# Two attention layers with a routed feed-forward: constants ahead of the statistics, the second late job's rows among the first one's gates, routing scatters one by one in two groups of four

## Chip, cores and metric

The kernel runs on one core of a Trainium2 chip. The metric is the device time of one execution in microseconds (us); lower is better. The core has a tensor engine (TensorE, PE in the profile; its weight loads are PEld), a vector engine (VectorE, DVE), a scalar engine (ScalarE, ACT), GpSimd (POOL) and a sync engine (SyncE, SP) that mostly issues DMAs. Each engine works through its own instruction list in order and waits on semaphores for the others. ScalarE, SP and GpSimd can issue DMAs; indirect ones, which take row numbers from a tile, are issued by GpSimd alone.

## What is computed

The reference, cut to what matters. `x` is (8, 512, 256) in float32, the context (8, 64, 256); there are 16 heads of 16, 8 experts with 1024 inner units and two experts for each token.

```python
x = x + L0_xattn(layernorm(x), ctx, ctx)       # 16 heads, softmax over 64 keys
x = x + L0_ffn(layernorm(x))                   # per batch, the 384 tokens with the highest
                                               # score get gelu(x @ w_block), the others pass
x = x + L1_xattn(layernorm(x), ctx, ctx, mask)
x = x + L1_ffn(layernorm(x))

def L1_ffn(hidden):                            # routed experts
    probs = softmax(x @ gate_w.T)
    w, idx = top_k(probs, 2); w = w / sum(w)
    for e in range(8):
        g, u = split(x @ gate_up[e].T)
        acc += combine[:, e] * ((silu(g) * u) @ down[e].T)
```

## The kernel before

The work has two halves. In the **front half** eight batches of 512 tokens go through a chain of steps each: attention 0, the token-choice layer, attention 2, and routing. A step is a Python closure that issues a few instructions on several engines, and a long string, `ORDER`, written out by hand, says which chain issues its next step: a digit 0 to 7 is the next step of that batch, a letter A to H the ranks of a batch, `s` the next setup step (constants, sorted by a number), `k` and `v` keys and values, `l` the job lists, `j` early expert jobs. `in_order` (L1215) ties every instruction behind the one before it on the same engine, so each engine's list follows `ORDER`. Only TensorE, VectorE, ScalarE and GpSimd are tied so; SP takes its DMAs in the order in which they are traced.

A normalisation (`norm_steps`, L375) has four steps. `stats` runs the statistics of four 128-token tiles on VectorE (L384, L385), adds eps (L387) and lets GpSimd raise to the power -0.5 (L389, `rstd`, with the constant `mhalf`). `scaled` makes `shift` on VectorE (L395) and four ScalarE activations (L398). Two `turned` steps transpose on TensorE (L413) against the constant `ident` and copy on ScalarE. Batch 0's chain needs these first; `keys` (L323, L331) needs the constant `headm`, which VectorE sums from `ownh` (L244). `mhalf`, `ownh`, `ident` and `minus` are made by GpSimd from nothing but fills and index patterns. GpSimd also issues the two loads of `bv`, the value biases, at the start of its list (L149), and adds the output bias `bo` to x (L435).

An attention's score part has a single PSUM buffer `ps_s`: `by_keys` fills `st` (L498, L506), two ScalarE exponentials `ex` (L515) empty it, and the next `st` can only then be filled. `by_tokens` uses the same buffer for `sc` (L466, L475), which VectorE's maximum (L482) empties.

Routing (`route_steps`, L698) ends in `placed`, which works out two slots for each token, and in four steps `sent_off(t)`, each with two indirect DMAs (L816, the "scatters"): 128 rows of 260 floats, from `xr` to the list `xs` in DRAM, for each token tile and each of the two choices. So a batch has eight. The last of a batch is made to wait until the other seven have landed and then stands for all, except in the last batch, whose eight are all waited for. Where `ORDER` has them, a batch's four steps stand next to each other or a few steps apart. Behind the scatters on GpSimd's list stand the next `rstd`s and `bo` additions.

Some experts' jobs run early (`early_steps`, L1069), woven into the last batches: rows and weights are loaded on SP, `gate_up` (L1138) and `down` (L1165) run on TensorE, and the rows are added to the output by indirect DMAs (`add_rows`, L106). Their first row load waits for the last scatter of batch 3.

In the **second half** 35 jobs follow (and a 36th if the counts need it), of three kinds: full (256 rows), one (128 rows), pair (two units of 64). For each the rows `xg` come by DMA (L1278), `enter` transposes them (L1318), copies `xjT` on ScalarE (L1320) and prepares tokens and weights on VectorE (L1324 to L1338); `gate_up_full` runs eight blocks of eight products each (L1349) with ScalarE's silu (L1357) and VectorE's product (L1358); `down` runs the second matrix (L1406) and adds the rows. For job i of the list, the gates come first, then `enter` of job i+1, then `down` of job i-1. At i = 0 there is no job before, so the transposes of job 1 stand directly ahead of job 1's gates. The steps of the first three jobs are tied by `in_order` too (`placed`, L1445). Job 0's rows are loaded behind its gate weights on SP and wait for all eight scatters of batch 7.

Of the kernel before, what the change touches and what calls it, by code (L numbers as in the profile page):

```python
# [47 lines left out]
NQ = P // QR  # L48

ORDER = """  # L50
sssss0sss0ksk0s1020001s0k110s1vs0s031010s7s2s40v320v2410030v20120ss01040502A010A30A0As10
1013010343201130005s12010sk0112151761Bs2B1BB112120241201v102s2050223s022302412C22123C2C0
21C02131012110323150030sv02411033123104102523105200004331323426D14D34Ds14D2341v233613421
63233344212345412615434311432513431414312E25124E544E452356E54722434237252346535264345645
256352452F362F2325F63F464556355473355463574536743566474353567335566346v37l64763G464jj77j
5jGj666j5j7jj47Gjjj765j7457j4G5j64654j7j6556747j5j76446444j4746sH6jj56j557j76j7j57jj7Hsj
76jjjjHH7565j65jj676jj7jj6j57j5j6j75557j555jj57j6j667j7jjjs67j66j76j7676j66j76s667j676jj
jj7jjj77j7j7jjjjj77jjs7j7j7j7j7j77jj7jjjljj7jj7jj
"""


# [1 line left out]
def xattn_ffn_kernel(ctx: ExitStack, tc: tile.TileContext, a: dict, out: bass.AP):  # L63
# [28 lines left out]
    def after(i, others):  # L92
        for other in others:
            tc.add_manual_dep(
                i, other.name,
                mybir.DependencyInfo(mybir.DependencyClass.Sync, mybir.DependencyReason.DATA),
                reason="rows that it needs",
            )

    def apart(i, others, reason):  # L100
        for other in others:
            tc.declare_no_dep(i, other, reason=reason)
# [14 lines left out]
    with ExitStack() as front:  # L117
# [36 lines left out]
        def load_layer(l, names, q):  # L154
            for n in names:
                how = load_mat if n[0] == "w" else load_col if n in ("bk", "bq") else load_row
                layers[l][n] = how(q, f"{n}{l}")
# [10 lines left out]
            q.dma_start(x_sb[:, t, :], x_t[0][:, t, :])  # L168
        load_layer(0, ("bk", "wv", "bq"), nc.scalar)
        load_layer(1, ("wv",), nc.sync)  # L170
        load_layer(0, ("bv",), nc.gpsimd)
        load_layer(1, ("bv",), nc.gpsimd)
        load_layer(0, ("wq", "bo", "wo"), nc.sync)
        nc.sync.dma_start(x_sb[:, TB : 2 * TB, :], x_t[1])
        load_layer(1, ("wk", "bk"), nc.sync)
# [42 lines left out]
        def within(at, name, shape, bounds, lasts=False):  # L218
# [12 lines left out]
            return v  # L231

        every = slice(0, P)
        mhalf = within(-0.9, "mhalf", [TB], [])
        setups.append((-0.89, lambda: nc.gpsimd.tensor_scalar_mul(mhalf, mhalf, -0.5)))

        ownh = within(
            -0.85, "ownh", [HC],
            [(ALU.is_ge, 0, [[-DK, HC]], 1), (ALU.is_ge, DK - 1, [[DK, HC]], -1)],
        )  # L240
        headm = const.tile([P, 2], F32, name="headm")
        setups.append((
            -0.84,
            lambda: nc.vector.tensor_reduce(  # L244
                headm, ownh.rearrange("p (r i) -> p i r", i=2), AX.X, ALU.add
            ),
        ))
        setups.append((-0.8, lambda: make_identity(nc, ident)))
        warm = const.tile([P, TB], F32, name="warm")
        setups.append((-0.895, lambda: nc.scalar.activation(warm, mhalf, AF.Exp)))  # L250

# [446 lines left out]
        def route_steps(b):  # L698
# [107 lines left out]
                    nc.vector.tensor_reduce(xr[:, :, D + col], part, AX.X, ALU.add)  # L806
                got["slots"] = slots

            def sent_off(t):
                slots, xr = got["slots"], got["xn"]  # L810

                sent = scattered.setdefault(b, [])
                for k in range(TOPK):
                    i = nc.gpsimd.indirect_dma_start(  # L816
                        out=xs,
                        out_offset=bass.IndirectOffsetOnAxis(ap=slots[:, t, k : k + 1], axis=0),
                        in_=xr[:, t, :],
                        in_offset=None,  # L820
                    ).ins
                    final = len(sent) == TB * TOPK - 1 and b < B - 1
                    if b >= B // 2:
                        apart(i, early_loads, "rows of other batches")
                    for other_i in sent:
                        if final:
                            tc.add_manual_dep(
                                i, other_i.name,
                                mybir.DependencyInfo(
                                    mybir.DependencyClass.Sync, mybir.DependencyReason.DATA  # L830
                                ),
                                reason="the last scatter stands for all",
                            )
                        else:
                            tc.declare_no_dep(i, other_i, reason="rows of their own")
                    sent.append(i)
                routed[:] = sent[-1:] if b < B - 1 else sent

            steps += [gates, logits, chosen, counted, weighed, placed]
            return steps + [lambda t=t: sent_off(t) for t in range(TB)]  # L840

# [225 lines left out]
        def early_steps(j):  # L1069
            got = {}  # L1070

            def load():
                if not e_w:
                    e_w["gu"] = wpool[0].tile([P, NC, 2 * FF], F32, tag="wgu", name="e_wgu")
                    e_w["dn"] = wpool[0].tile([P, NF, D], F32, tag="wdn", name="e_wdn")
                with tc.issue_after(last.pop().ins) if last else nullcontext():
                    row = nc.sync.value_load(
                        jobs_early[0:1, 0, j : j + 1], min_val=0, max_val=E * QROWS - P
                    )
                    e = nc.sync.value_load(jobs_early[0:1, 1, j : j + 1], min_val=0, max_val=E - 1)  # L1080
                i = nc.sync.dma_start(
                    e_xg, xs[bass.ds(row, 2 * P), :].rearrange("(s p) w -> p s w", p=P)
                ).ins
                early_loads.append(i)

                for b in scattered:
                    if b >= B // 2:
                        apart(i, scattered[b], "rows of other batches")
                after(i, scattered[B // 2 - 1][-1:])
                got["e"] = e  # L1090

            def load_piece(n):
# [117 lines left out]
            mybir.EngineType.PE, mybir.EngineType.DVE, mybir.EngineType.Activation,  # L1210
            mybir.EngineType.Pool,
        )
        behind = {}

        def in_order(step):  # L1215
            traced = nc.cur_bb.bb.instructions
            last = traced[-1].name
            step()
            made = []
            for i in reversed(nc.cur_bb.bb.instructions):  # L1220
                if i.name == last:
                    break
                made.append(i)
            for i in reversed(made):
                if i.engine not in engines:
                    continue
                ahead = behind.setdefault(i.engine, [])
                for other in ahead:
                    tc.add_manual_dep(
                        i, other,  # L1230
                        mybir.DependencyInfo(
                            mybir.DependencyClass.NoSync, mybir.DependencyReason.DATA
                        ),
                        reason="the order of the steps",
                    )

                if "DMA" not in type(i).__name__:
                    ahead.clear()
                ahead.append(i.name)
# [98 lines left out]
        nc.vector.tensor_tensor(wt[:, 0:subs], wt[:, 0:subs], wt2[:, 0:subs], ALU.add)  # L1338
        return xT, tok, wt

    def gate_up_full(j, xT, w):
        wgu = w[0][0]
        hT = moe.tile([P, NF, 2 * P], F32, tag="hT", name=f"hT_{j}")
        for f in range(NF):
            ps = ps_gu.tile([P, 2, 2 * P], F32, tag="gu", name=f"gu_{j}_{f}")
            for half in range(2):
                o = half * FF + f * P
                for c in range(NC):
                    nc.tensor.matmul(  # L1349
                        ps[:, half, :],  # L1350
                        lhsT=wgu[:, c, o : o + P],
                        rhs=xT[:, c].rearrange("p s q -> p (s q)"),
                        start=(c == 0),
                        stop=(c == NC - 1),
                    )
            sg = moe.tile([P, 4 * P], F32, tag="sg", name=f"sg_{j}_{f}")
            nc.scalar.activation(sg[:, 0 : 2 * P], ps[:, 0, :], AF.Silu)  # L1357
            nc.vector.tensor_tensor(hT[:, f, :], sg[:, 0 : 2 * P], ps[:, 1, :], ALU.mult)  # L1358
        return hT
# [94 lines left out]
    for i, j in enumerate(order):  # L1454
        w = loads.pop(0)[1]
        xT, tok, wt = entered.pop(0)
        if i > 0:
            loads.append(load_at(i + 2))
        if j < NLATE:
            hT = placed(i, lambda: gate_up_full(j, xT, w))  # L1460
        else:
            h, hT = placed(i, lambda: gate_up_rows(j, xT, w))
        if i == 0:
            small_list()
            unit_list()
            loads.append(load_at(2))
        if i + 1 < len(order):
            entered.append(placed(i, lambda: enter(order[i + 1], loads[0][0])))
        if pending is not None:
            placed(i, lambda: down(*pending))  # L1470
        if j >= NLATE:
            placed(i, lambda: turn(j, h, hT))
        pending = (j, hT, w, tok, wt)
# [55 lines left out]
```

## Time and profile before

| | us |
|---|---|
| median of 3 runs | 1176.1 |
| lowest and highest run | 1172.63, 1177.84 |
| the profiled execution | 1176.21 |
| its span, first to last instruction | 1174.5 |
| TensorE busy in it | 1145.1 |

The profile is one execution. Its page gives each engine's busy time, a row of 40 equal slices for each engine (a digit is tenths of busy time), and the costliest groups of instructions. A line of a group reads: source line, engine, operation, out<-in, count, then busy time and mean duration in ns, then the engine's idle time just before these instructions and what ended most of it. A line of the timeline reads: start in us, duration in us, engine, line, operation, out<-in, count; in brackets the idle time before it and what released it. Several equal instructions in a row are merged into one line. A line of the list of waits reads: who waited for whom, total us, how often, and the longest.

How long the groups that the change touches take:

```profile
L816 POOL DMA_INDIRECT xs<-xr,slots x64 | 63.0, 984 | 102.4 <-issue 62.5
L389 POOL TENSOR_TENSOR rstd<-ve,mhalf 128x4 f32<-128x4 f32 x32 | 33.2, 1037 | 231.8 <-DVE ve L387 180.3
```

### The profile page before, as it was taken

Reading aid. Unit: us, or ns where it says so; the run is one execution under the profiler, and the core shown is the slowest. Engines: PE = TensorE matmul, PEld = TensorE weight load, DVE = VectorE, ACT = ScalarE, POOL = GpSimd, SP = SyncE. Lnnn points to the kernel's source line nnn. Section 1 sums busy time; section 2 is a strip of 40 time slices with the busy share of each in tenths; the row PEclk is TensorE's granted clock in tenths of the full one; section 3 lists DMA queues with packets and bytes.
Section 4 is the critical chain, followed back from the end, with each engine's and each line's share of the span. In section 5 each row is a group of like instructions: output and inputs, shape, how many; then the busy total and the mean of one; then the engine's idle time right before and its main releaser. Section 6 shows DMA issues by size and latency. Waiting matters only on the chain. (4 is left out here: it accounts for less than half of the span.)

```text
span 1174.5 us, 20888 instructions
## 1 busy us (share of the span) xinstructions
PE 1145.1 (97%) x8010; PEld 823.9 (70%) x8010; DVE 575.8 (49%) x1664; ACT 372.7 (32%) x713; POOL 282.7 (24%) x308
## 2 busy tenths in 40 slices
PE   7999999999999999999999999999999999999997
PEld 3656665656567777778887876777767777677786
DVE  6898887878887676645822221222212222222211
ACT  3655654645553433222121111221111211212210
POOL 5331134123340321431422112112121121211212
PEclk9999999999999999999999999999999999999999
DMA  9000001010115444445799688896889967987811
GB/s 269 2 1 2 1 20 38 19 56 20 37 62 182 116 129 119 138 142 163 220 340 308 251 283 301 294 317 225 295 283 329 311 214 274 312 310 237 279 14 19
DMA packets 119988, 203.53 MB, mean 173 GB/s; under 512 B 10608, under 2 KB 105712, under 8 KB 108368
## 3 DMA queue, kind: packets, MB, share of 16 engines
q1 hardware_dynamic: 100048, 179.35, 43.6%
q0 software_dynamic: 14496, 17.86, 7.5%
q10 hardware_dynamic: 5344, 4.98, 1.3%
q8 instruction: 64, 1.05, 0.4%
q14 instruction: 36, 0.29, 0.1%
HBM read 180.38 MB, written 23.47 MB: 174 GB/s over the span
## 5 line engine op out<-in xcount | busy, mean ns | idle before, releaser
L1349 PE MATMUL gu<-xjT,wgu 128*128 128x256 f32 x1152 | 252.1, 379 | 1.3 <-ACT xjT L1320 1.3
L1349 PEld LDWEIGHTS gu<-xjT,wgu 128*128 128x128 f32 x1152 | 217.6, 190 | 31.9 <-ACT xjT L1320 1.8
L106 POOL DMA_INDIRECT out_dram<-now,tok x63 | 98.0, 1556 | 476.1 <-DVE now L1414 286.9
L1406 PE MATMUL o<-wdn,hT 128*128 128x256 f32 (+1 forms) x1008 | 189.2, 380 | 0.0
L1406 PEld LDWEIGHTS o<-wdn,hT 128*128 128x128 f32 (+1 forms) x1008 | 151.1, 173 | 28.3 <-issue 1.7
L1358 DVE TENSOR_TENSOR hT<-sg,gu 128x256 f32<-128x256 f32 x144 | 60.6, 421 | 192.1 <-ACT sg L1357 189.4
L1357 ACT ACTIVATE sg<-gu 128x256 f32<-128x256 f32 x144 | 55.2, 383 | 209.5 <-PE gu L1349 202.8
L1376 PE MATMUL gr<-wgu,xjT 128*64 128x512 f32 (+1 forms) x432 | 120.8, 596 | 0.0
L1138 PE MATMUL gu_e<-x_sb,e_wgu 128*128 128x256 f32 x448 | 101.6, 382 | 0.6 <-ACT x_sb L1117 0.6
L1138 PEld LDWEIGHTS gu_e<-x_sb,e_wgu 128*128 128x128 f32 x448 | 83.8, 190 | 15.5 <-issue 2.6
L1414 DVE TENSOR_SCALAR now<-o,wt 128x256 f32<-128x256 f32 x53 | 25.6, 483 | 139.8 <-PE o L1406 139.8
L1376 PEld LDWEIGHTS gr<-wgu,xjT 128*64 128x64 f32 (+1 forms) x432 | 42.8, 150 | 68.4 <-issue 67.0
L389 POOL TENSOR_TENSOR rstd<-ve,mhalf 128x4 f32<-128x4 f32 x32 | 33.2, 1037 | 231.8 <-DVE ve L387 180.3
L816 POOL DMA_INDIRECT xs<-xr,slots x64 | 63.0, 984 | 102.4 <-issue 62.5
L482 DVE TENSOR_REDUCE mx<-sc 128x32 f32<-128x2048 f32 x32 | 73.2, 2288 | 21.4 <-PE sc L475 18.3
L1386 DVE TENSOR_TENSOR h<-sg,gr 128x512 f32<-128x512 f32 x34 | 23.3, 687 | 82.6 <-PE gr L1376 82.6
L445 PE MATMUL ps_q<-xT,w_wq 128*128 128x512 f32 x128 | 63.4, 624 | 0.3 <-ACT xT L416 0.2
L576 PE MATMUL py<-w_wo,cT 128*128 128x256 f32 x256 | 60.4, 384 | 1.1 <-DVE cT L565 1.1
L1385 ACT ACTIVATE sg<-gr 128x512 f32<-128x512 f32 x34 | 20.3, 597 | 124.7 <-PE gr L1376 124.7
L576 PEld LDWEIGHTS py<-w_wo,cT 128*128 128x128 f32 x256 | 47.2, 190 | 13.1 <-issue 5.3
L398 ACT ACTIVATE xn<-x_sb,shift,rstd 128x256 f32<-128x256 f32 x96 | 49.8, 594 | 17.3 <-DVE shift L395 16.0
L384 DVE BATCH_NORM_STATS2 st<-x_sb 128x6 f32<-128x256 f32 x128 | 51.3, 401 | 3.9 <-DMA x_sb<-in_x_dram 3.8
(287 smaller groups left out, 1451.9 us busy)
## 6 DMA issues: line engine op xcount, KB each, us to landing
wgu<-in_guT_dram SPq DMA_DIRECT2D x90, 1024.0 KB
wdn<-in_dnT_dram SPq DMA_DIRECT2D x45, 1024.0 KB
e_wgu<-in_guT_dram SPq DMA_DIRECT2D x56, 256.0 KB
e_wdn<-in_dnT_dram SPq DMA_DIRECT2D x7, 1024.0 KB
xg<-xs SPq DMA_DIRECT2D x18, 260.0 KB
out_dram<-x_sb ACTq DMA_DIRECT2D x8, 512.0 KB
x_sb<-in_x_dram SPq DMA_DIRECT2D x7, 512.0 KB
x_sb<-xs SPq DMA_DIRECT2D x7, 260.0 KB
```

Of the source, the lines that this page charges most:

```text
L106: i = nc.gpsimd.indirect_dma_start(out=out_rows, out_offset=bass.IndirectOffsetOnAxis(ap=tok, axis=0), in_=rows, in_offset=None, bounds_ch ...
L384: nc.vector.bn_stats(st, x_sb[:, b * TB + t, :])
L445: nc.tensor.matmul(ps, lhsT=w["wq"][:, k, c * P : (c + 1) * P], rhs=got["xT"][:, k, :], start=(k == 0), stop=(k == NC - 1),)
L482: nc.vector.tensor_reduce(got["mx"].rearrange("p t (r h) -> p r t h", r=NQ)[:, :, :, 2 * c : 2 * c + 2], sc, AX.X, ALU.max,)
L576: nc.tensor.matmul(py[:, s, :], lhsT=cT[:, c, t * P : (t + 1) * P], rhs=w["wo"][:, c, :], start=(c == 0), stop=(c == NC - 1),)
L816: i = nc.gpsimd.indirect_dma_start(out=xs, out_offset=bass.IndirectOffsetOnAxis(ap=slots[:, t, k : k + 1], axis=0), in_=xr[:, t, :], in_of ...
L1138: nc.tensor.matmul(ps[:, half, :], lhsT=e_w["gu"][:, c, o : o + P], rhs=e_xT[:, c].rearrange("p s q -> p (s q)"), start=(c == 0), stop=(c ...
L1349: nc.tensor.matmul(ps[:, half, :], lhsT=wgu[:, c, o : o + P], rhs=xT[:, c].rearrange("p s q -> p (s q)"), start=(c == 0), stop=(c == NC - 1),)
L1357: nc.scalar.activation(sg[:, 0 : 2 * P], ps[:, 0, :], AF.Silu)
L1358: nc.vector.tensor_tensor(hT[:, f, :], sg[:, 0 : 2 * P], ps[:, 1, :], ALU.mult)
L1376: nc.tensor.matmul(ps[rows], lhsT=xT[:, c, 0, rows], rhs=wgu[:, c, o : o + 4 * P], start=(c == 0), stop=(c == NC - 1),)
L1406: nc.tensor.matmul(ps[rows], lhsT=hT[:, f, s * P + rows.start : s * P + rows.stop], rhs=wdn[:, f, :], start=(f == 0), stop=(f == NF - 1),)
```

## The change

1. `mhalf` becomes one fill with -0.5 instead of a fill with 1 and a multiplication. `ownh`, `headm` and `ident` get smaller sort numbers, and `ORDER` begins with seven setup steps instead of five, so these come ahead of batch 0's statistics; the memset of the first `mx` stays ahead of them too. The two loads of `bv` become a setup step behind the statistics, on GpSimd. The scaling of `bq` moves behind `scaled` and the first `keys`.
2. `sent_off` takes one choice k, so a batch has eight steps with one scatter each. `ORDER` has them as two groups of four; the first group stands where the first of the four old steps stood, the second some steps later (batch 7: four pairs, where its four steps stood). Every scatter waits for the last TensorE instruction issued before its step (`products`). The first scatter of a batch waits for all eight of the batch before; none waits for another of its own batch. What waited for a batch's last scatter waits for all eight.
3. At i = 0 the first four gate blocks are issued, then `enter` of job 1, then the other four; `enter` is not issued again behind them.

In `ORDER`, apart from the scatters, only those two setup steps at the start move.

```diff
-sssss0sss0ksk0s1020001s0k110s1vs0s031010s7s2s40v320v2410030v20120ss01040502A010A30A0As10
+sssssss0s0ksk0s1020001s0k110s1vs0s031010s7s2s40v320v2410030v20120ss01040502A010A30A0As10
...
-21C02131012110323150030sv02411033123104102523105200004331323426D14D34Ds14D2341v233613421
...
+21C02131012110323150030sv024110331231041025231052000043313234260000D14D34Ds14D2341v23361
...
-        load_layer(0, ("bv",), nc.gpsimd)
-        load_layer(1, ("bv",), nc.gpsimd)
...
-        mhalf = within(-0.9, "mhalf", [TB], [])
-        setups.append((-0.89, lambda: nc.gpsimd.tensor_scalar_mul(mhalf, mhalf, -0.5)))
+        mhalf = const.tile([P, TB], F32, name="mhalf")
+        setups.append((-0.9, lambda: nc.gpsimd.memset(mhalf, -0.5)))
+        setups.append((
+            -0.855, lambda: [load_layer(l, ("bv",), nc.gpsimd) for l in range(2)]
+        ))
 
         ownh = within(
-            -0.85, "ownh", [HC],
+            -0.88, "ownh", [HC],
...
-            -0.84,
+            -0.87,
             lambda: nc.vector.tensor_reduce(
                 headm, ownh.rearrange("p (r i) -> p i r", i=2), AX.X, ALU.add
             ),
         ))
-        setups.append((-0.8, lambda: make_identity(nc, ident)))
+        setups.append((-0.865, lambda: make_identity(nc, ident)))
...
-            def sent_off(t):
+            def sent_off(t, k):
                 slots, xr = got["slots"], got["xn"]
                 sent = scattered.setdefault(b, [])
-                for k in range(TOPK):
...
-                    final = len(sent) == TB * TOPK - 1 and b < B - 1
...
+                if sent:
+                    apart(i, sent + scattered.get(b - 1, []), "rows of their own")
+                elif b > 0:
+                    after(i, scattered[b - 1])
+                sent.append(i)
+
+                if products:
+                    after(i, products[-1:])
+                routed[:] = sent
...
-            return steps + [lambda t=t: sent_off(t) for t in range(TB)]
+            return steps + [
+                lambda t=t, k=k: sent_off(t, k) for t in range(TB) for k in range(TOPK)
+            ]
...
-                after(i, scattered[B // 2 - 1][-1:])
+                after(i, scattered[B // 2 - 1])
...
+                if i.engine == mybir.EngineType.PE:
+                    products[:] = [i]
...
-    def gate_up_full(j, xT, w):
+    def gate_up_full(j, xT, w, hT=None, chunks=range(NF)):
         wgu = w[0][0]
-        hT = moe.tile([P, NF, 2 * P], F32, tag="hT", name=f"hT_{j}")
-        for f in range(NF):
+        if hT is None:
+            hT = moe.tile([P, NF, 2 * P], F32, tag="hT", name=f"hT_{j}")
+        for f in chunks:
...
-        if j < NLATE:
+        if i == 0:
+
+            hT = placed(i, lambda: gate_up_full(j, xT, w, None, range(NF // 2)))
+            entered.append(placed(i, lambda: enter(order[1], loads[0][0])))
+            placed(i, lambda: gate_up_full(j, xT, w, hT, range(NF // 2, NF)))
+        elif j < NLATE:
...
-        if i + 1 < len(order):
+        if 0 < i < len(order) - 1:
             entered.append(placed(i, lambda: enter(order[i + 1], loads[0][0])))
```

## The prediction

> **What bounds the kernel now.** I read the page first (engine shares, then the 40 slices), then TensorE's list of waits, then the order in time around each of its gaps.
>
> ```profile
> PE 1145.1 (97%) x8010; PEld 823.9 (70%) x8010; DVE 575.8 (49%) x1664; ACT 372.7 (32%) x713; POOL 282.7 (24%) x308
> ...
> PE   7999999999999999999999999999999999999997
> ```
>
> TensorE is busy 97% of the span and nearly full in every slice but the first and the last. The change leaves TensorE's instructions as they are; one group of four transposes changes its place. So it can only win back gaps, and TensorE's idle time is 1174.5 - 1145.1 = 29.4 us, of which 5.0 us pass before the first weights land and about 7.4 us after the last product. The rest is small, and TensorE's waits say for whom:
>
> ```profile
> PE st L498 <- ACT ex L515: 4.3, 3, 2.4
> PE ps_x L413 <- ACT xn L398: 3.2, 3, 2.9
> PE gu L1349 <- ACT xjT L1320: 1.3, 2, 0.7
> ```
>
> (Total, times, longest.) The second is at the start, the third at the first two late jobs, and the first lies where routing scatters run. The change has a part for each.
>
> **Part 1, constants ahead of the statistics.** The first normalisation in time:
>
> ```profile
> 8.43 0.43 DVE L384 BATCH_NORM_STATS2 st<-x_sb 128x6 f32<-128x256 f32 x1 [1.74 <-DMA x_sb<-in_x_dram]
> ...
> 10.49 1.06 POOL L389 TENSOR_TENSOR rstd<-ve,mhalf 128x4 f32<-128x4 f32 x1 [2.24 <-DVE ve L387]
> ...
> 12.17 0.16 DVE L244 TENSOR_REDUCE headm<-ownh 128x2 f32<-128x8 f32 x1 [1.19 <-POOL ownh L225]
> 12.25 0.15 DVE L395 SCALAR_TENSOR_TENSOR shift<-mv,rstd 128x4 f32<-128x4 f32 x1
> ...
> 13.24 0.73 PE L413 MATMUL ps_x<-ident,xn 128*128 128x128 f32 x2 [2.92 <-ACT xn L398]
> ...
> 15.63 5.11 PE L445 MATMUL ps_q<-xT,w_wq 128*128 128x512 f32 x8
> ```
>
> rstd is ready at 11.55, but shift starts at 12.25: headm stands ahead of it on VectorE and waits for ownh, which GpSimd makes behind rstd. In the new order ownh, ident and headm come before the statistics (GpSimd is free until 10.49 apart from fills), and the bq scaling (10.80, after 0.47 of waiting) comes behind shift. Shift can then start near 11.6: 0.65 us. Further, the two 128 KB loads of bv go from GpSimd's start (1.36) to behind the first rstd. They move in the stretch in which the statistics wait for x. At that stretch's 267 GB/s, 256 KB are 0.98 us; I take 0.7, since not all of it runs ahead of x. Together 1.35 at the transposes. If the gap of 2.92 shrinks, the clock may also stay up: the 8 products at 15.63 take 5.11 us, and 4 of the same kind take 1.98 at 25.67, so 1.15 more could be had. But what follows caps it: VectorE starts batch 1's statistics at 15.40 as x lands, and the maximum that ends at 28.09 releases the transposes at 28.59, with 0.5 us to spare. I take **-1.3**; ends -0.6 and -2.2. The price of the move: two bv issues (1.33 us) stand behind rstd on GpSimd, ahead of minus. Minus is wanted at 30.14 and bv at 28.71, and before, the loads had landed some 7 us after issue, so both are covered by some 8 us; without that cover each late us would be one us. SP's queue is not touched.
>
> **Part 2, the scatters.** Each batch has 8 indirect DMAs of about 0.96 us plus 0.30 between them, back to back for the most part, the last held until the others have landed. Two samples:
>
> ```profile
> 186.85 1.04 PE L506 MATMUL st<-mxT,minus 32*128 32x512 f32 x8
> ...
> 187.89 1.22 POOL L816 DMA_INDIRECT xs<-xr,slots  x1 [0.30 <-DMA xs<-xr,slots]
> ...
> 190.19 1.94 ACT L515 ACTIVATE ex<-st 128x1024 f32<-128x1024 f32 x2 [3.33 <-PE pf L660]
> ...
> 192.18 1.75 PE L498 MATMUL st<-qT,kbd 32*128 32x512 f32 x8 [2.37 <-ACT ex L515]
> 193.68 1.95 PE L506 MATMUL st<-mxT,minus 32*128 32x512 f32 x8
> ```
>
> ```profile
> 236.57 1.07 PE L475 MATMUL sc<-kbd,qT 32*128 32x128 f32 x32
> ...
> 239.92 2.29 DVE L482 TENSOR_REDUCE mx<-sc 128x32 f32<-128x2048 f32 x1 [2.89 <-PE py L576]
> ```
>
> The scores are complete at 187.89 and ScalarE, free since 186.86, takes them up at 190.19, 2.3 us late. VectorE takes up at 239.92 what was complete at 237.64, again 2.3 late. Elsewhere such a hand-over takes about 0.1 us (31.18 to 31.25 in the same pair of lines). So while scatters run, an engine learns late of another's result. Why, the trace does not tell; that it comes with the scatters, it does. All gaps of TensorE over 0.4 us between 50 and 540 us lie in scatter stretches: 2.37 (before 192.18), 0.97 (242.27), 1.65 (247.84), 1.05 (297.15), 0.68 (344.16), 1.03 (517.54), 1.14 (522.82), in sum 8.89. After the first, the products run slow: 1.75, 1.95 and 1.25 against 1.14, 1.04 and 1.06 elsewhere, 1.7 us more, with a granted clock of 0.56 in that stretch.
>
> By the Trainium skill, page "TensorE: Matmul & The Clock Gate", section "Part 1: The HAM clock gate", the clock is halved after a whole idle window of about 3.4 us. By that rule a gap of 2.37 us would cost nothing beyond itself and this 1.7 would drop out of the saving; the slow rows above say that here it does cost.
>
> The new order issues four, lets GpSimd and TensorE go on, and issues four more behind a named product; only a batch's first scatter waits for landings, those of the batch before, some 50 us old. A group of four lasts 4 x 1.26 = 5.0 us, and a scatter lands 1.2 to 1.9 us after its issue (the waits of the last ones: 1.73 to 1.90), so a group is over after about 6.2 us, against over 10 for eight. Counted from the start of its batch's scatters, the late hand-over lies at 7.8 us (2.37 gap), 8.5 (1.65), 7 to 9 (1.05), 8.9 (1.03 and, following from it, 1.14): 7.24 us of gaps, which a group of four does not reach. It lies at 1.9 us (0.97) and 4.8 us (0.68) for the other 1.65, which stay. The second groups are new and bring gaps of that early kind; since each stands right ahead of the next softmax product, I charge them twice, 3.3. Net: -7.24 - 1.7 + 3.3 = **-5.6**. Ends: -10.6 (all 8.89 and 1.7 go) and +10.6 (rival B). The new wait for a product holds GpSimd's queue: behind it stand rstd (L389), the bo additions (L435) and, among early jobs, the row additions (L106). They had stood behind all 8 and the held last one (1.73 to 1.9 of waiting), so most come earlier; I cost this at nothing.
>
> Batch 7 has four pairs as before, but the last pair now waits for the last gate product of the last early job (576.7 instead of 572.09). It ends near 579.0 and lands at 580.3 to 580.9; the first late job's rows, issued on SP at 579.98, wait for it, and behind them on SP stand that job's wdn and the next job's loads, which are not yet due. The rows were wanted at 583.67 with little to spare. **+0.5**, ends 0 and +1.0.
>
> **Part 3, the second late job's rows.** Its transposes end at 599.47 and its gates start at 600.14, after ScalarE's copy (0.58). Placed after four of the first job's eight gate blocks, the copy lies under 6.9 us of products; its rows had landed by 587.91 (GpSimd's zero rows, which wait for them, start there) and the new place is near 592. **-0.65** (one of the two waits of 1.3 in all); ends -0.68 and 0.
>
> **Sum**: -1.3 - 5.6 + 0.5 - 0.65 = -7.05. The span 1174.5 becomes 1167.4. The profiled execution took 1176.2, 1.7 more than its span, and the median is 1176.1, so I set it against that: **1169.0 us**.
>
> **Rivals.** A: the late hand-overs do not hang on how many scatters run in a row. Then part 2 moves gaps and wins nothing: -1.3 + 0.5 - 0.65 = -1.45, 1174.6. For it: lateness began 1.9 us into batch 1's scatters. Against: in batch 0 all was punctual for 5 us and more. It is also the case if the split does not part the groups: in batch 0 only four additions (2.85 us) lie between, and in batch 3 nothing, since the product named there ends at 335.98, before its first four are out. B, slower: lateness comes with each group's start, whatever its length. Eight batches cost 10.6 us now, 1.32 each; 16 groups would cost 21.2, so +10.6 - 1.45 = +9.15, 1185.2. It decides from about 14 groups on (18.5 - 10.6 - 1.45 = +6.4). For it: the early cases, and that a second group stands ahead of a chain scores, exponentials, scores with one buffer. Against: five of the seven gaps came late in their stretch. C: all scatter gaps go, -10.6 - 1.45: 1164.1; against it, the early cases keep their place.
>
> **How the numbers follow.** Forecast 0.55 (own range 1165.5 to 1172), C 0.08, A 0.25, B 0.12. A measurement here can tell about 0.5%, 5.9 us, so faster means below 1170.2: four fifths of the forecast and C, 0.53. Within: the rest of the forecast and A, 0.35. Slower: B, 0.12. The range reaches from below C to A's far side with the wait of the last pair at its worst and a few second groups as in B: 1163 to 1179.
>
> **What would show it.** The first transposes start near 11.9 instead of 13.24, with shift right behind rstd. No wait of L498 over 1 us near 190 and 247, and no slice of halved clock after 20 us. The gap at 600 is gone. SP issues the first late rows at 580.4 or later. I am wrong if TensorE's gaps in the scatter stretches sum to over 6 us, or a second group has a gap over 2 us.

## The result, and the profile after

| | before | after |
|---|---|---|
| median, 22 runs each | 1176.1 us | 1172.9 us |
| ratio, 95% interval | | 0.9974 (0.9968 to 0.998) |
| span of the profiled execution | 1174.5 | 1171.5 |
| TensorE busy in it | 1145.1 | 1146.6 |
| last product ends at | 1167.1 | 1164.2 |

The change wins 3.1 us by the ratio, less than half of the 7.1 forecast; the interval excludes 1. The page's first line and TensorE's list of waits, after (total, times, longest):

```profile
PE 1146.6 (98%) x8010; PEld 825.0 (70%) x8010; DVE 574.6 (49%) x1664; ACT 372.9 (32%) x713; POOL 283.5 (24%) x307
```

```profile
...
PE ps_x L414 <- ACT xn L399: 2.3, 7, 1.3
PE sc L467 <- ACT ex L516: 1.6, 4, 0.9
PE st L499 <- DVE mx L483: 1.5, 1, 1.5
PE ps_x L1317 <- DMA xg<-xs: 0.8, 1, 0.8
PE ps_x L414 <- ACT xr L399: 0.7, 4, 0.2
PE gu L1349 <- ACT xjT L1319: 0.7, 1, 0.7
...
```

The wait for `ex` that led the list before (4.3 us) is nearly gone and one of the two waits for `xjT` with it. New are the waits for `xr` and for `xg`, and the wait for `xn` at the start is still 2.3 us. TensorE is also busy 1.5 us longer with the same 8010 instructions, so some products run slower; gaps alone don't tell the whole loss.

Since TensorE's order is nearly the same, each product can be set against itself. This table (start of the same product after, less its start before) shows where time is won and given back:

| start before | what | after - before |
|---|---|---|
| 13.24 | batch 0's first transpose | -2.43 |
| 18.35 | batch 0's queries | -3.67 |
| 25.45 | batch 0's scores | +0.24 |
| 195.56 | behind batch 0's scatters | -3.35 |
| 242.27 | `st` in batch 1's | -2.45 |
| 247.84 | `st`, 6 us on | -3.91 |
| 253.72 | scores, 6 us on | -1.64 |
| 297.15 | in batch 2's | -3.27 |
| 349.88 | behind batch 3's | -1.72 |
| 488.66 | batch 6's routing transposes | +0.15 |
| 522.82 | behind batch 6's | -3.06 |
| 583.67 | first late job's transposes | -2.00 |
| 600.14 | second late job's gates | -2.81 |

**The start** wins 3.67 us and gives all of it back by 26 us. The timeline after:

```profile
9.96 0.16 DVE L396 SCALAR_TENSOR_TENSOR shift<-mv,rstd 128x4 f32<-128x4 f32 x1 [1.16 <-POOL rstd L390]
...
10.81 0.33 PE L414 MATMUL ps_x<-ident,xn 128*128 128x128 f32 x1 [0.16 <-ACT xn L399]
...
14.16 0.43 DVE L385 BATCH_NORM_STATS2 st<-x_sb 128x6 f32<-128x256 f32 x1 [1.07 <-DMA x_sb<-in_x_dram]
...
18.11 0.43 DVE L385 BATCH_NORM_STATS2 st<-x_sb 128x6 f32<-128x256 f32 x1 [1.52 <-DMA x_sb<-in_x_dram]
...
20.45 0.16 DVE L396 SCALAR_TENSOR_TENSOR shift<-mv,rstd 128x4 f32<-128x4 f32 x1
...
21.30 0.33 PE L414 MATMUL ps_x<-ident,xn 128*128 128x128 f32 x1 [1.29 <-ACT xn L399]
...
24.03 2.03 PE L476 MATMUL sc<-kbd,qT 32*128 32x128 f32 x32
```

`shift` follows `rstd`, and the transposes start at 10.81. But the second `shift` (batch 1's, 20.45) stands on VectorE's list behind batch 2's statistics, and these wait until 18.11 for batch 2's x. TensorE stands still from 20.01 to 21.30, and from 22.45 to 25.86 the granted clock is 0.5: the 32 small products at 24.03 take 2.03 us against 1.17 for batch 0's (16.92).

**The scatters** after, in batch 1:

```profile
239.82 1.14 PE L499 MATMUL st<-qT,kbd 32*128 32x512 f32 x8 [1.46 <-DVE mx L483]
...
249.01 0.95 PE L476 MATMUL sc<-kbd,qT 32*128 32x128 f32 x10
250.17 0.52 PE L476 MATMUL sc<-kbd,qT 32*128 32x128 f32 x5 [0.20 <-issue]
250.91 0.51 PE L476 MATMUL sc<-kbd,qT 32*128 32x128 f32 x6 [0.22 <-issue]
251.64 0.71 PE L476 MATMUL sc<-kbd,qT 32*128 32x128 f32 x11 [0.22 <-issue]
```

and, in batch 5's second group, which ends at 483.38:

```profile
482.42 0.96 POOL L816 DMA_INDIRECT xs<-xr,slots  x1 [0.30 <-issue]
...
486.68 2.07 ACT L399 ACTIVATE xr<-x_sb,shift,rstd 128x256 f32<-128x256 f32 x4 [5.06 <-DMA xs<-xr,slots]
487.33 0.33 PE L414 MATMUL ps_x<-ident,xr 128*128 128x128 f32 x1 [0.20 <-ACT xr L399]
487.83 0.33 PE L414 MATMUL ps_x<-ident,xr 128*128 128x128 f32 x1 [0.16 <-ACT xr L399]
```

32 scores that take 1.07 us elsewhere are spread over 3.3 us (249.01 to 252.35), and the profile shows nothing that they wait for ("issue"). And ScalarE stands for 5.06 us until scatters have landed: `xr`, the rows that they read, has one buffer, and the next batch's routing activation overwrites it. The transposes that were ready before then trickle in one by one, 0.49 us apart.

### The profile page after: what moved, and what is told of

Read it like the earlier page. It is cut to its first block, busy times and chain, and to the rows that moved or that the text cites. A ratio compares the mean times of both kernels' runs of the same rounds, so it can differ in the third digit from the quotient of the medians.

```text
span 1171.5 us, 20900 instructions
## 1 busy us (share of the span) xinstructions
PE 1146.6 (98%) x8010; PEld 825.0 (70%) x8010; DVE 574.6 (49%) x1664; ACT 372.9 (32%) x713; POOL 283.5 (24%) x307
```

## Experiments

Each group of runs was made on one chip, one after the other, with the kernel before among them. These groups differ more than the kernels do: in some the kernel before takes 1175 to 1176 us, as in the comparison above, in others 1164 us. The expectations call this a matter of the chip. Here the first kind is called a **late** group and the second a **punctual** one, after the late hand-overs; the last section says more of it.

| run | edit | group (before, us) | us | ratio, 95% interval |
|---|---|---|---|---|
| e1 | before + start | late (1176.0) | 1175.3 | 0.9996 (0.9983 to 1.0008) |
| e2 | before + scatters | late | 1173.3 | 0.9975 (0.9966 to 0.9984) |
| e3 | after, statistics of batch 2 later | late | 1170.4 | 0.9954 (0.9941 to 0.9967) |
| e4 | after, bv behind x | late | 1169.1 | 0.9948 (0.9935 to 0.996) |
| e5 | after, eight in one run | punctual (1164.7) | 1164.4 | 0.9997 (0.9988 to 1.0006) |
| e6 | after, four pairs | punctual | 1163.2 | 0.9994 (0.9985 to 1.0003) |
| e7 | after, batch 7 free | punctual | 1165.4 | 1.0007 (0.9998 to 1.0016) |
| e8 | after, no product wait | punctual | 1163.1 | 0.999 (0.9979 to 1.0002) |
| e10 | after itself | punctual (1164.1) | 1165.5 | 1.0016 (1.0007 to 1.0024) |
| e11 | as e4 | punctual | 1163.7 | 0.9994 (0.9985 to 1.0002) |
| e12 | as e5 | punctual | 1164.7 | 1.0002 (0.9993 to 1.001) |
| e13 | pairs, bv behind x, batch 7 free | late (1174.8) | 1163.9 | 0.9903 (0.9888 to 0.9918) |
| e14 | eight in one run, else as e13 | late | 1182.3 | 1.0063 (1.005 to 1.0077) |
| e15 | as e6 | punctual (1164.4) | 1164.2 | 0.9995 (0.9986 to 1.0004) |
| e16 | after itself | punctual | 1166.0 | 1.0012 (1.0003 to 1.0021) |
| e17 | as e13 | punctual | 1161.3 | 0.9974 (0.9964 to 0.9983) |
| e18 | as e6 | late (1175.8) | 1166.5 | 0.9925 (0.9912 to 0.9939) |

### The start: e1 to e4

e1 is the kernel before with the change's first part alone, e2 with its second alone.

> The kernel before with part 1 alone (constants ahead of the statistics, bv's loads behind the first rstd). Theory now: batch 0's transposes start near 10.8 us and TensorE is some 3.5 us ahead by batch 0's queries, but batch 1's shift stands on VectorE behind batch 2's statistics, which wait for batch 2's x (18.1 us, 1.4 later than before, because bv's 256 KB now run ahead of it); so a gap of about 1.3 us before batch 1's transposes, a half-clock stretch near 22 us, and from 26 us on everything as before or 0.3 us later: ratio to before 1.000 (0.9995 to 1.0005). Rival, the prediction's term: -1.3 us, ratio 0.9989. If it is -3 us, the loss in the full change comes from its other parts.

> The kernel before with part 2 alone (scatters one by one in two groups of four, each behind the last product traced before it). Theory now: TensorE's gaps and slow stretches near 190, 247, 296 and 517 to 522 us go (about 9 us), but the second groups cost some 6 us instead of the 3.3 forecast, and the first late job's rows come about 1 us later: -2 to -2.8 us in all, ratio 0.998. The prediction's terms: -5.6 + 0.5 = -5.1 us, ratio 0.9957. Rival A (lateness doesn't hang on the number in a row): 0 to +0.5 us, ratio 1.000.

Both medians lie where the theory put them. In e1 TensorE is 3.98 us ahead at the queries and 0.9 us ahead from 24 us on; no half clock fell into its start after 11 us. How the clock's windows fall makes one profile a poor measure here. Against before, the products at 100 us lie between 0.9 us ahead (e9) and 1.4 us behind (e2) in the three traces with the unchanged start, 0.2 us behind on average. In the eleven traces with the change's own start they lie between 1.9 us ahead (e12) and 1.7 us behind (e16), 0.8 us ahead on average; the three that are behind (after, e7, e16) are those with half clock after 20 us. So the start wins some 1.0 us on average, on few traces. The median of e1 gives -0.5 us, with an interval that reaches from -2.0 to +0.9 and does not exclude -1.3. e2 is clearer: its -2.7 us exclude the -5.1 of the prediction's terms (0.9957). So it is no interplay of the parts that costs most of the rest.

e3 moves batch 2's statistics (the digit 2) behind batch 0's second score step:

```diff
-sssssss0s0ksk0s1020001s0k110s1vs0s031010s7...
+sssssss0s0ksk0s100001s0k1102s1vs0s031010s7...
```

> The changed kernel with batch 2's first statistics moved in the hand-written order from ahead of batch 1's shift to behind batch 0's second score step. If batch 2's x holds batch 1's shift: batch 1's transposes follow the keys at about 20 us without the gap of 1.3 us, no half clock after 20 us, and from 33 us on TensorE is 1.5 to 2.5 us ahead of the changed kernel; ratio to before 0.9974 - 0.0017 = 0.9957 (0.9950 to 0.9963). If the start is bound elsewhere (VectorE's maxima, the loads in general): the gap moves to another place, ratio 0.9974 as the changed kernel.

e4 leaves the order and moves bv's loads on SP's list:

```diff
         for b in range(2, 4):
             nc.sync.dma_start(x_sb[:, b * TB : (b + 1) * TB, :], x_t[b])
+        for l in range(2):
+            load_layer(l, ("bv",), nc.sync)
...
-        setups.append((
-            -0.855, lambda: [load_layer(l, ("bv",), nc.gpsimd) for l in range(2)]
-        ))
```

> The changed kernel with bv's two loads on SP behind the x of batches 2 and 3 instead of on GpSimd behind the first rstd. If bv's 256 KB are what makes batch 2's x late: it lands near 17 us instead of 18.1, batch 1's shift comes about 0.7 to 1.1 us earlier, the gap before batch 1's transposes shrinks from 1.3 to 0.2 to 0.6 us, and the half clock may go too: 0.7 to 2 us less, ratio 0.9957 to 0.9968. If bv's place is without effect: ratio 0.9974 as the changed kernel. If bv lands too late for the values at 28.7 us, a new wait there: ratio over 0.9974.

The timeline of e4:

```profile
13.58 0.43 DVE L384 BATCH_NORM_STATS2 st<-x_sb 128x6 f32<-128x256 f32 x1 [0.89 <-DMA x_sb<-in_x_dram]
...
15.92 0.42 DVE L384 BATCH_NORM_STATS2 st<-x_sb 128x6 f32<-128x256 f32 x1
...
18.25 0.15 DVE L395 SCALAR_TENSOR_TENSOR shift<-mv,rstd 128x4 f32<-128x4 f32 x1
...
19.41 0.50 PE L413 MATMUL ps_x<-ident,xn 128*128 128x128 f32 x2
```

Batch 2's statistics (15.92) no longer wait for x, batch 1's `shift` is there at 18.25 instead of 20.45, and the transposes follow without a gap; no half clock comes after the first 8 us. Either edit keeps what the start wins: 2.3 us (0.9974 - 0.9954) and 3.1 us (0.9974 - 0.9948) below the changed kernel. So it was batch 2's x that held batch 1, and bv's 256 KB that made it late.

### The scatters, in punctual groups: e5 to e12

e5 puts the eight scatters of batches 0 to 6 in one run where the first group of four stood, e6 makes four pairs of them, spread to where the second group stood. For batch 0 (the zeros in a row):

```diff
-21C02131012110323150030sv024110331231041025231052000043313234260000D14D34Ds14D2341v23361
+21C02131012110323150030sv024110331231041025231052000000004331323426D14D34Ds14D2341v23361
...
-21C02131012110323150030sv024110331231041025231052000043313234260000D14D34Ds14D2341v23361
+21C02131012110323150030sv024110331231041025231052004330013230042600D14D34Ds14D2341v23361
```

> The changed kernel with the eight scatters of batches 0 to 6 in one run, where its first group of four stands; still one by one, still each behind the last product traced before it, none held for the others' landing. If the late hand-overs grow with the number in a row: TensorE's gaps of 1 to 2.4 us come back late in the stretches (near 190, 245, 295 and 517 to 522 us, 5 to 8 us in all), while what the second groups cost (6 us) goes: ratio to before 0.998 to 1.000. If the number in a row has no part in it (rival A): gaps as in the changed kernel or fewer, ratio 0.9974 or below, down to 0.993. In both cases ScalarE no longer waits for landed scatters at its routing activation near 483 to 487 us, and the 2.0 us lost there come back.

> The changed kernel with four groups of two in batches 0 to 6, spread evenly from the place of the first group of four to that of the second. If lateness grows with the number in a row: the gap of 1.46 us near 238, that of 0.86 us near 347 and the slow products near 250 us (2.1 us) go, the last pair lands 2.5 us earlier than the second group and ScalarE's wait near 483 us shrinks: 3 to 5 us less than the changed kernel, ratio to before 0.993 to 0.995. If each group's start costs something whatever its length (rival B): 14 more groups at 0.4 to 1.3 us, 6 to 18 us more, ratio 1.002 to 1.013.

e7 and e8 take away the wait for a product, in batch 7 or everywhere:

```diff
-                if products:
+                if products and b < B - 1:
                     after(i, products[-1:])
```

> The changed kernel without the wait for a product in batch 7's scatters alone. If that wait delays the first late job's rows: they land 0.8 to 1 us earlier and TensorE's gap of 0.79 us ahead of that job's transposes goes: ratio to before 0.9974 - 0.0007 = 0.9967. If the rows come late for another reason (that job's 2 MB of weights beside them): the gap stays, 0.9974.

> The changed kernel with no scatter waiting for a product: GpSimd issues each as soon as its list comes to it. If the wait is what parts the two groups: they close up (batch 0 has only four additions between them, batch 3 nothing), late gaps of 1 to 2 us return and the ratio to before is 0.998 to 0.999, though batch 7's rows come 0.8 us earlier. If the order of GpSimd's list parts them anyway: gaps as in the changed kernel, ratio 0.9967 to 0.9974.

None of the four told what it was made for, since none of their traces shows a gap of over 0.5 us between 50 and 540 us, whatever the grouping. So the next group held both kernels again.

> The kernel before itself, unchanged, once more, for its trace on the chip of this group of runs. In the last group the times lay near 1164 us, the kernel before among them (1164.7), and no trace of it had a gap of over 0.3 us in a scatter stretch, with two groups, four, or one: so late hand-overs would be the chip's and not the kernel's. Then this run is either near 1176 us with the gaps near 190, 242, 247, 296, 344, 517 and 522 us (8.9 us in all), or near 1164.7 us without them; a time near 1164.7 with these gaps, or 1176 without, would speak against it.

The kernel before took 1163.7 us. Its timeline where the trace of before had its longest gap:

```profile
185.96 1.04 PE L506 MATMUL st<-mxT,minus 32*128 32x512 f32 x8
...
187.00 1.21 POOL L816 DMA_INDIRECT xs<-xr,slots  x1 [0.30 <-DMA xs<-xr,slots]
187.06 1.94 ACT L515 ACTIVATE ex<-st 128x1024 f32<-128x1024 f32 x2 [1.10 <-PE st L506]
...
189.05 1.14 PE L498 MATMUL st<-qT,kbd 32*128 32x512 f32 x8
```

The same scatters run at the same pace, and ScalarE takes the scores up at 187.06, as soon as they are complete, not 2.3 us later. All seven gaps over 0.5 us (8.89 us) are gone from the same program.

> The changed kernel itself once more. On a chip with late hand-overs: ratio 0.9974 as first measured, gaps of 1.46 us near 238 and 0.86 near 347. On a chip without: nothing is left for the scatters' part to win, the start gives +0.3 us, the second late job's place -0.7, the first late job's rows +0.8, sum +0.4 us: ratio 1.000 to 1.001, no gap over 0.5 us between 50 and 540 us.

> The changed kernel with bv's loads on SP behind the x of batches 2 and 3, once more. On a chip with late hand-overs 0.9948 as before. On one without: the start wins some 3.4 us and the second late job's place 0.7, the first late job's rows cost 0.5 to 0.8: -3.3 us, ratio 0.997.

> The changed kernel with the eight scatters of batches 0 to 6 in one run, none held, once more, in case this chip has late hand-overs: then gaps of 1 to 2.4 us late in the stretches and a ratio of 0.998 to 1.000 if lateness grows with the number in a row, 0.9974 or below if it doesn't. On a chip without late hand-overs: no such gaps, 0.9997 as before.

In a punctual group the change makes the kernel slower: 1.0016, a little over the expected 1.000 to 1.001, and 1.0012 in e16. Product by product against e9: the start -0.4 us, the routing transposes of batch 6 +1.7, the first late job's rows +1.1, the second late job -0.8; sum +1.6, the difference of the two spans (1163.6 and 1162.0). The +1.7 is in the main the wait for `xr`: its activation starts at 478.72 behind scatters, and in e9 at 475.74. With eight in one run (e12) it isn't there. e11 missed its 0.997: its start wins 1.9 us on that of e9, not 3.4, and it keeps the wait for `xr`.

e7 left a gap of 0.63 us at the first late job, e8 none. In all runs without the wait for a product batch 7's last scatter is issued 3.3 us behind that job's gate weights; the last of its packets ended 8.8 to 9.1 us behind them in before, e1, e8 and e9, and 10.1 to 10.7 us in e7, e13, e14 and e17. With the wait (e10) it is issued at 8.7 and has landed at 10.8. In all eight traces without the wait a 16 KB packet of the instruction queue lies nearby. In the four that land late the last scatter packet ends 0.45 to 1.04 us behind it (in e7 the packet runs from 569.64 to 570.58, the scatters until 571.30); in the four that land early it ends while that packet runs. The trace does not tell which DMA engine carries a packet, so it isn't shown that one holds up the other. Taking the wait away brought the rows early in e8 and not in e7.

### The scatters, in late groups: e13 to e18

> The changed kernel with three edits together: bv's loads on SP behind the x of batches 2 and 3, four groups of two scatters in batches 0 to 6, no product wait in batch 7. On a chip without late hand-overs, from the places of single edits there: start -1.9 us, no wait at the routing activations (0 instead of +1.7), first late rows 0 instead of +0.9, second late job -0.8: -2.7 us, ratio 0.9977. On a chip with them (the kernel before near 1176 us): if lateness grows with the number in a row, nearly all of the 10.6 us of gaps and slow products go: -13 us, ratio 0.989; if each group's start costs (rival B): over 0.995.

> The same with the eight scatters of batches 0 to 6 in one run instead of four pairs. On a chip without late hand-overs: as with pairs, 0.9977, within 0.0005 of it. On a chip with them: if lateness grows with the number in a row, gaps late in the stretches as in the kernel before (up to 8.9 us and 1.7 us of slow products stay): ratio 0.996 to 0.998, 5 us or more over the pairs; if the number has no part in it, as with pairs.

These two differ only in where `ORDER` has the scatters of batches 0 to 6, and ran in one late group: 1163.9 and 1182.3 us. e14 was expected at 0.996 to 0.998 and came out slower than the kernel before. TensorE's gaps of over 0.5 us between 50 and 540 us are one of 0.91 us with pairs and nine of 14.6 us in sum with eight in one run. The timeline of e14 in batch 0's run:

```profile
183.91 1.04 PE L506 MATMUL st<-mxT,minus 32*128 32x512 f32 x8
...
188.68 1.94 ACT L515 ACTIVATE ex<-st 128x1024 f32<-128x1024 f32 x2 [4.76 <-remote]
...
190.67 1.14 PE L498 MATMUL st<-qT,kbd 32*128 32x512 f32 x8 [3.80 <-ACT ex L515]
```

The scores end at 184.95, ScalarE takes them up at 188.68, 3.7 us late ("remote" is the profile's word for a release that it can't name). With groups of four (the changed kernel) two gaps of 2.3 us in sum are left, with eight and the last one held (before) seven of 8.9 us.

The pairs are pairs in `ORDER`, not all in time: where GpSimd has nothing else to do between them, they close up. In e13 the scatters run two by two in batches 1 and 6, six and two in batches 0 and 5, four and twice two in 2 and 4, and all eight in a row in batch 3, where the changed kernel's two fours close up too. The first and the last of e13's six in batch 0, which follow each other 0.30 us apart, and the gap behind them:

```profile
177.22 1.22 POOL L815 DMA_INDIRECT xs<-xr,slots  x1 [6.44 <-DVE xr L806]
...
183.81 0.98 POOL L815 DMA_INDIRECT xs<-xr,slots  x1 [0.30 <-issue]
...
187.81 1.14 PE L498 MATMUL st<-qT,kbd 32*128 32x512 f32 x8 [0.91 <-ACT ex L515]
```

The pairs' gaps of over 0.5 us lie at these long runs alone: 0.91 us at batch 0 in e13, 0.89 at batch 0 and 0.86 at batch 3 in e18. So in a late group the loss grows with the number in a row, and starting a group costs little: e13 has 19 groups in batches 0 to 6, the changed kernel 13. The number isn't all, though: e14's eights in batches 4 and 5 leave no such gap. Pairs also stand elsewhere beside the other engines' work than a run of eight, and number and place were not varied apart.

> The changed kernel with four groups of two as its only edit. On a chip with late hand-overs (the kernel before near 1176 us): the second groups' losses and the gap near 238 go, some 6 us less than the changed kernel, ratio 0.992; if the pairs' gain in the last group of runs came from bv's place and batch 7 alone, 0.9974 less at most 0.003. On a chip without (near 1164 us): 0.9994 as before, only the wait at the routing activations gone.

> The changed kernel itself, beside the pairs on one chip. With late hand-overs 0.9974, without 1.0016, as measured before; if it came out near the pairs on a chip with late hand-overs, groups of four would do as well.

> Pairs, bv's loads behind the x of batches 2 and 3, batch 7 without the product wait, once more. With late hand-overs 0.990, 2 us or more below the pairs alone; without them 0.9977 (-2.7 us), and not above 1.000.

> The changed kernel with four groups of two as its only edit, a third time. On a chip with late hand-overs (the kernel before near 1176 us): 0.992 if the pairs carry most of the 0.9903 of the version with all three edits, 0.9945 or above if bv's place and batch 7 carry half of it. On a chip without them 0.9995 as before, and the question stays open.

e15 to e18 came out as expected. The pairs alone give 0.9925 in a late group against 0.9974 for the fours, and 0.9994 and 0.9995 in punctual ones against 1.0016 and 1.0012. With bv's loads behind x and batch 7 free the ratio is 0.9903 (late) and 0.9974 (punctual): the version of e13 and e17 beats both kernels in both kinds of group, by 10.9 and 3.1 us on before.

## Why the prediction was wrong, step by step

**Bound.** Right: TensorE's work is the span, and only gaps and slow products can be won. Of the 4.0 us that the forecast missed by, 2.3 are part 2's and 0.6 batch 7's; nearly all the rest is the start's in this profile.

**Part 1, -1.3 us.** Came out as +0.3 in the profile of after, -0.4 in e10 against e9, -0.5 in the median of e1 and about -1.0 on average over all traces, inside its ends of -0.6 and -2.2; so its size is not refuted, and the profile of after is one with half clock. The first steps were right, and stronger than said: `shift` right behind `rstd`, transposes at 10.81 against 11.9. What failed is the step "what follows caps it", which put the cap at batch 1's statistics and at the maximum that ends at 28.09. The cap lay between the two: batch 1's `shift` stands behind batch 2's statistics, and bv's loads, taken out ahead of batch 0's x, now ran ahead of batch 2's. I had priced the moved loads by their readers and by GpSimd's queue, not by whose transfer they push back. e3 and e4 each take that wait away and get 2.3 and 3.1 us more, and in a punctual group e11 gets 2.6 us more than e10 (1.0016 - 0.9994).

**Part 2, -5.6 us.** In the table above, -3.3. Its mechanism held, in late groups: fewer scatters in a row bring fewer late hand-overs (e13 against e14), and the gaps near 190, 247, 297 and 517 to 522 went, with them the half clock behind the first. The gains are 10.5 us (3.59 + 1.46 + 1.63 + 0.62 + 3.21; the 0.62 lies at 344 us, between two rows of the table), more than the 8.9 taken and as much as rival C's 10.6. The mis-sized term is "second groups charged 3.3": the losses are 7.2 us. Of these 0.9 lie between batch 0's second group and batch 1's first, and 0.9 and 1.2 at batches 2 and 3: together 3.1, about the 3.3 charged, though batch 3's two groups ran as one run of eight, as the prediction feared under rival A. The rest was not in the sum at all: 2.3 us of scores that run slowly in batch 1's second group, a loss that makes no long gap and stands with the same 2.3 us in the traces of e2, e3 and e4 (why they run slowly stays open), and 1.9 us by batch 6's routing transposes, in the main where ScalarE waits for landed scatters before it may overwrite `xr`. I had named what stands behind the scatters on GpSimd's list, but not who needs the buffer that they read. A second buffer for `xr` was not tried.

**The early and the late gap.** I was to be wrong if the gaps in the scatter stretches summed to over 6 us or a second group had one over 2 us. Neither happened (2.3 us in gaps over 0.5 us), and the sum was wrong all the same: the test looked at gaps, and most of the 7.2 us were not in long ones.

**Batch 7, +0.5 us.** Right in kind, measured +1.06, a little over its end of +1.0. With the wait the last scatter lands 1.8 us later (e10 10.8 against e9 9.0 us behind the gate weights).

**Part 3, -0.65 us.** Measured -0.8, a little over its end of -0.68; the gap at 600 is gone.

**The clock.** "No slice of halved clock after 20 us" was wrong, as the stretch at 22.45 shows; see the last section for the rule.

**Rivals.** A (lateness doesn't hang on the number in a row) and B (lateness with each group's start) fall with e13 against e14, with the reserve that a scatter's place changed with its group. A gave 1174.6 and lies nearer to the measured time than the forecast, for a reason that wasn't its own. And the ground itself was not the kernel's alone: in punctual groups there is no lateness to remove, and the change costs 1.4 to 1.9 us there by the ratios. The 0.5% that the prediction took a measurement to tell was too coarse: the interval is 0.06% to either side.

## What to carry to other kernels

When a load moves, ask whose bytes now come behind it, and when a reader of a buffer moves later, ask who is waiting to overwrite that buffer; both cost more here than the queues that the change touched. Set equal products of two traces against each other rather than summing gaps, since a loss can hide in products that merely run slowly. Before explaining a wait by the kernel, run the unchanged kernel again in another group of runs: an 11 us effect of this one comes and goes with the group of runs. And see in the trace whether instructions that the order sets apart run apart.

## What was not expected of the hardware

**Late and punctual groups.** The kernel before took 1174.8 to 1176.1 us in four groups, the first comparison among them, and 1164.1 to 1164.7 us in three, with every execution of a group on the same side (1172.6 to 1178.3 and 1162.7 to 1169.2). The difference of some 11 us is about the 10.6 us of late hand-overs and slow products that the trace of before shows. It isn't a fixed property of a chip, as the expectations put it: under one and the same chip number runs were punctual in e9 to e12 and in e15 to e17 and late in e18. The scatters themselves take 984 ns each in before and in e9.

The traces differ in one more thing. The profile's list of DMA issues ends with the median time from issue to landing. In all eleven punctual traces it has one for the scatters; in all nine late ones it has none for any DMA. Before and e9:

```profile
xs<-xr,slots POOLq DMA_INDIRECT x64
xs<-xr,slots POOLq DMA_INDIRECT x64, 2.8
```

It can't match landings because records of them are missing: the traces of late groups hold 6038 to 6299 records of semaphore steps that came from DMAs, those of punctual groups 7005 to 7023. Between 150 and 200 us, where batch 0's eight scatters and one other DMA land, there are 70 in before and 144 in e9. So one trace tells which kind of group it is from. Whether what loses the records also delays the hand-overs, and what makes a group late, stays open.

**The clock.** The granted clock changes in steps of 3.41 us. Setting TensorE's idle time in each such window against the clock of the next, over all traces here and all windows before the last product that ran at full clock themselves: after all eight windows with 1.96 us or more idle the next ran at half clock, after all but one of those with 1.52 us or less at full clock, and between 1.59 and 1.84 us it was half in three cases and full in three. The Trainium skill, page "TensorE: Matmul & The Clock Gate", section "Part 1: The HAM clock gate", has the clock halved after a whole idle window of about 3.4 us; the traces agree with the window's length and not with the need for a wholly idle one.
